# A step size that is written in place in PSUM, multiplied there, and then copied to SBUF

## The chip, the core and the metric

The kernel runs on one core of a Trainium2 chip. The metric is the device time of one execution in microseconds (us). Four runs of the kernel before took 8771.61 to 8812.8 us, with a median of 8785.41 us. The engines are named as in the profile: PE (TensorE, matrix multiply), DVE (VectorE), ACT (ScalarE), POOL (GpSimd) and SP (SyncE, which here only issues transfers).

## What is computed

Four images of 96 channels and 64 x 64 pixels pass through four layers: a selective state space model over the pixels (layer 0), a deformable convolution (layer 1), a Fourier layer and a feed-forward network (layer 2), and a linear attention with another feed-forward network (layer 3). The change lies in layer 0. Its core, cut from the reference:

```python
delta = softplus(dts + delta_bias)          # the step size, (batch, 4, 192, 4096)
# for every pixel, in each of 4 directions k:
dA = exp(delta[..., None] * A)              # A: 16 states for each of 192 channels
h  = dA * h + (delta * u)[..., None] * B
y  = einsum('bkdn,bkn->bkd', h, C)          # + D * u
```

`dts` is a small linear map of the layer's convolved input u. Two results of the step size are needed: delta itself, for the decay dA, and the product delta * u, for the inflow. The four directions are rows and columns, each forward and backward.

## The kernel before

**The scan.** `Layer0.scan` (L884) goes through 1536 units: image, direction, block of 1024 pixels, group of channels. For each unit, 8 channels by 16 states lie on the 128 partitions. ACT makes the decay `da` with an exponential (L1000) from a broadcast load of delta (L979); PE spreads the product into a PSUM tile `db` (L1006); DVE multiplies db by B (L1020, in place in PSUM) and runs the recurrence (L1028); POOL multiplies by C (L1037); PE sums over the states into `py` (L1056). A few units are in flight at a time.

**Beside the scan.** Everything else is written as Python generators and is put between the scan's instructions. There are two streams. Stream 0 (`ends`) makes the inputs of layer 0 for images 0 to 3 (`first`, `before`), and then takes each image through layers 2 and 3: Fourier layer (two halves, each hidden, transforms, and "last", L1576 to L1583), feed-forward network ("FFN", 8 chunks, L1643 to L1681), attention, FFN. Stream 1 (`middle`) finishes layer 0 of each image (`behind`) and does layer 1 (`Layer1`; the sampling gathers pixels with L1369 and ends in the matmuls L1402 and L1418). Image b can enter layer 2 only when stream 1 has sampled it.

**What sets the order.** A planner decides at build time what stands beside which unit. Each generator yields steps with an estimated work per engine (`cost(dve=0.7)`), and `pipe` (L273) lets a chain go on when the engines have room by its own clock (`Clock`). Steps can take and free named tiles (`takes`, `frees`), and can say that they hold a PSUM bank (`holds=1`). Beside the scan there are three banks for all streams (pool `mm`), and `has_bank` (L393) starts no new chain that needs a bank while three are held. The instructions of every engine then run in the order in which they were written out, each waiting only for its data. After the last unit the scan's banks are given to stream 0 (`own_banks`), and what is left of both streams is written out without a scan beside it. In that part the FFN uses DVE for its conversions; beside the scan it uses ACT and POOL.

**The step size.** `Layer0.steps` (L810) is called 192 times: 4 images, 8 pieces of 512 pixels, 6 combinations of directions and channels. Each call:

- L827: PE makes dts in the bank `pd` (128 x 512, one bank).
- L829 to L833: ACT makes exp(-|dts|) in `ex`, log(1 + ex) in `lw`, and 1 + ex in `w1`.
- L836: DVE forms the rounding error of 1 + ex; L838: POOL corrects lw with it.
- L840: DVE makes the step size max(dts, 0) + lw from pd and lw, and writes it to the SBUF tile `rl`. This is the last reader of pd, and the bank is free after it.
- L846 and L847, L853 or L859: DVE multiplies rl by u into ex. 64 calls are plain (L859, u in `xa`), 48 take the channels 128 to 191 of a row and a column direction (L859, u in `xc`), 16 take those of one orientation in two halves (L846, and L847 with u read with a stride), and 64 read u with a stride as columns (L853).
- L862: SP issues the store of rl to DRAM, from where L979 loads it later.
- L866 to L876: ex is split into three bf16 parts, by ACT and by PE with a bank `pr` (L869, L870, L873), and L880 stores them. The scan's `db` comes from these.

`pd`, `pr` and the banks of all other chains beside the scan are the same three banks in turn.

Of the kernel before, what the change touches and what calls it, by code (L numbers as in the profile page):

```python
# [15 lines left out]
ALU = mybir.AluOpType  # L16
# [3 lines left out]
B, C, H, W = 4, 96, 64, 64  # L20
# [163 lines left out]
def cost(pe=0.0, dve=0.0, act=0.0, pool=0.0, **more):  # L184
    return Step((pe, dve, act, pool), **more)


def wait(us=0.0, **more):

    return Step((0.0,) * 4, us, **more)  # L190
# [75 lines left out]
class Chain:  # L266
    def __init__(self, steps, ready):
        self.steps, self.ready = steps, ready
        self.done, self.holds, self.new, self.takes = 0, 0, True, []
        self.kind = steps.gi_code  # L270


def pipe(net, chains, width, every=0, lane=None, **tiles):  # L273
# [5 lines left out]
    while True:  # L279
        if more and len(active) < width:  # L280
            steps = next(chains, None)
            if steps is None:
                more = False
            else:
                active.append(Chain(steps, clock.now()))
                continue
# [256 lines left out]
class Layer0:  # L543
# [266 lines left out]
    def steps(self, b, ks, j, us, dtw, sm, xdbl):  # L810

        net = self.net
        nc = net.nc
        cs = slice(j * CH, (j + 1) * CH)
        tk = f"{b}_{j}_" + "".join(str(k) for k in ks)
        both = len(ks) == 2

        def tile_of(name, bufs):
            return sm.tile([128, CH], F32, name=f"{name}{tk}", tag=name, bufs=bufs)

        yield wait(new=True, takes="ex lw")


        pd = net.mm(f"pd{tk}")
        for i, k in enumerate(ks):
            o, m = (pd[64 * i : 64 * i + 64], slice(128, DI)) if both else (pd, slice(0, 128))
            nc.tensor.matmul(o, lhsT=dtw[:, k, m], rhs=xdbl[k % 2, j], start=True, stop=True)  # L827
        ex = tile_of("ex", 3)
        nc.scalar.activation(ex, pd, AF.Abs)  # L829
        nc.scalar.activation(ex, ex, AF.Exp, scale=-1.0)  # L830
        lw, w1 = tile_of("lw", 1), tile_of("w1", 1)
        nc.scalar.activation(lw, ex, AF.Ln, bias=net.one)
        nc.scalar.activation(w1, ex, AF.Identity, bias=net.one)  # L833
        yield cost(pe=2.2 if both else 1.1, act=2.7, holds=1, takes="rl")
        rl = tile_of("rl", 2)
        nc.vector.scalar_tensor_tensor(w1, w1, -1.0, ex, ALU.add, ALU.subtract)  # L836
        yield cost(dve=0.7, holds=1)
        nc.gpsimd.tensor_sub(lw, lw, w1)  # L838
        yield cost(pool=1.3, holds=1)
        nc.vector.scalar_tensor_tensor(rl, pd, 0.0, lw, ALU.max, ALU.add)  # L840
        yield cost(dve=0.7, frees="lw")
        if both and ks[0] % 2 == ks[1] % 2:
            q, xc = ks[0] % 2, us[2]
            own, far = slice(64 * q, 64 * q + 64), slice(64 - 64 * q, 128 - 64 * q)
            turned = xc.rearrange("p (a b) -> p b a", a=64)
            nc.vector.tensor_mul(ex[own], rl[own], xc[own, cs])  # L846
            nc.vector.tensor_mul(  # L847
                ex[far].rearrange("p (a b) -> p a b", b=64),
                rl[far].rearrange("p (a b) -> p a b", b=64),
                turned[far, j * NR : (j + 1) * NR, :],  # L850
            )
        elif not both and ks[0] % 2:
            nc.vector.tensor_mul(  # L853
                ex.rearrange("p (w h) -> p w h", h=H),
                rl.rearrange("p (w h) -> p w h", h=H),
                us[1][:, j * NR : (j + 1) * NR, :],
            )
        else:
            nc.vector.tensor_mul(ex, rl, us[2 if both else 0][:, cs])  # L859
        parts = ((0, 64, ks[0], 128), (64, 128, ks[1], 128)) if both else ((0, 128, ks[0], 0),)  # L860
        for p0, p1, k, c0 in parts:
            nc.sync.dma_start(self.de_d[b][k][c0 : c0 + p1 - p0, cs], rl[p0:p1])  # L862
        yield cost(dve=0.7, takes="du", frees="rl")

        du = sm.tile([128, 3, CH], BF16, name=f"du{tk}", tag="du", bufs=2)
        nc.scalar.copy(du[:, 0, :], ex)  # L866
        yield cost(act=0.6, new=True)
        pr = net.mm(f"pr{tk}")
        nc.tensor.matmul(pr, lhsT=net.ident, rhs=ex, start=True, stop=False)  # L869
        nc.tensor.matmul(pr, lhsT=self.minus, rhs=du[:, 0, :], start=False, stop=True)  # L870
        nc.scalar.copy(du[:, 1, :], pr)
        yield cost(pe=1.5, act=0.6, holds=1, frees="ex")
        nc.tensor.matmul(  # L873
            pr, lhsT=self.minus, rhs=du[:, 1, :], start=False, stop=True, skip_group_check=True
        )
        nc.scalar.copy(du[:, 2, :], pr)  # L876
        yield cost(pe=0.4, act=0.6)
        for p0, p1, k, c0 in parts:
            dst = self.du_d[b][k][:, c0 : c0 + p1 - p0, cs]
            nc.sync.dma_start(dst.rearrange("s c t -> c s t"), du[p0:p1])  # L880
        self.ready.update((b, k, both, j) for k in ks)
        yield wait(frees="du")
# [979 lines left out]
```

## Time and profile before

| What | Value |
|---|---|
| Four runs, median | 8785.41 us |
| Profiled execution | 8801.28 us, its span 8799.5 us |
| Granted TensorE clock | 0.811 |
| PE busy | 6636.2 us (75%) |
| DVE busy | 6852.6 us (78%) |
| ACT busy | 4917.9 us (56%) |
| POOL busy | 5605.5 us (64%) |
| First and last L1028 begin | 200.8 and 7491.4 us |

The profile is of one execution. It gives for each engine the time in which it was busy, in slices of the span and in any stretch; groups of instructions by source line, with their shape, their count, the mean duration, and what ended the idle time before them; and a chain of waits that leads back from the last instruction. A wait is put down to whatever released it last. DVE is the busiest engine, but no engine is busy all the time, and the part up to 7494 us, with the scan, is unlike the part behind it.

### The profile page before, as it was taken

What the parts mean: (1) busy time and instruction counts of PE and PEld (TensorE: products, weight loads), DVE (VectorE), ACT (ScalarE), POOL (GpSimd) and SP (SyncE); (2) the same over time, 40 slices, a digit from 0 to 9 for tenths busy, and PEclk for the clock granted to TensorE, in tenths of its full rate; (3) what the DMA queues carried; (4) which work ended last, traced back from release to release, by engine and by line L of the source; (5) the groups of instructions that cost most, each with busy time, mean ns of one, the idle gap of its engine ahead of it and who ended that gap; (6) DMA issues with size and microseconds to landing.
All of it is one profiled execution on the core that took longest, in us unless ns stands there. A gap on an engine that the chain in (4) does not pass through costs nothing.

```text
span 8799.5 us, 96335 instructions
## 1 busy us (share of the span) xinstructions
PE 6636.2 (75%) x31960; PEld 2923.1 (33%) x31960; DVE 6852.6 (78%) x5155; ACT 4917.9 (56%) x9030; POOL 5605.5 (64%) x4291
## 2 busy tenths in 40 slices
PE   6765877678777777887666787877768887778697
PEld 2211221123232232221222354422325552367383
DVE  2799989989798988778999887788888778367414
ACT  4554566546577776555666765445676565322323
POOL 0565666666588887656688886666888776177000
PEclk8876887779787887877788788877878887888887
DMA  3566677877788888777788888767888787255110
GB/s 86 168 197 188 180 195 216 212 183 195 196 233 238 242 232 208 191 177 190 212 236 221 234 223 200 183 166 185 216 209 230 202 215 163 58 167 168 30 52 11
DMA packets 775990, 1608.41 MB, mean 183 GB/s; under 512 B 247809, under 2 KB 339357, under 8 KB 773382
## 3 DMA queue, kind: packets, MB, share of 16 engines
q10 hardware_dynamic: 244224, 843.17, 37.1%
q1 hardware_dynamic: 457542, 532.51, 22.4%
q0 software_dynamic: 73728, 226.57, 9.7%
q8 instruction: 257, 4.21, 0.2%
q14 instruction: 239, 1.96, 0.1%
HBM read 1345.62 MB, written 256.29 MB: 182 GB/s over the span
## 4 chain that ended last, share of the span: by engine, by line
PE 34%; DVE 30%; DMA 16%; ACT 8%; issue 7%; POOL 2%; SPq 1%; ACTq 1%; DVEq 0%; POOLq 0%
DVE hh L1028 15%; DVE db L1020 8%; DMA du<-du 4%; PE py L1056 4%; PE pc L750 4%; PE f L1496 3%; PE ps L1402 3%; PE db L1006 3%; DMA da<-de 2%; PE pd L1418 2%; ACT g L1381 2%; ACT da L1000 2%; DMA bc<-bcd 1%; PE h L1537 1%; PE py L1051 1%
## 5 line engine op out<-in xcount | busy, mean ns | idle before, releaser
L1037 POOL TENSOR_TENSOR hh<-hh,bc 128x1024 f32<-128x1024 f32 x1536 | 3658.7, 2384 | 384.8 <-DVE hh L1028 278.7
L1028 DVE TENSOR_TENSOR_SCAN hh<-da,st,db 128x1024 f32<-128x1024 f32 x1152 | 2701.1, 2345 | 192.5 <-PE py L1056 74.1
L1020 DVE TENSOR_TENSOR db<-db,bc 128x1024 f32<-128x1024 f32 x1536 | 1863.3, 1213 | 577.2 <-PE db L1006 575.9
L1000 ACT ACTIVATE da<-da,w_al 128x1024 f32<-128x1024 f32 x1536 | 1740.1, 1145 | 614.6 <-DMA da<-de 182.3
L1006 PE MATMUL db<-du,rep 96*128 96x512 bf16 x3072 | 1098.4, 446 | 890.4 <-DVE hh L1028 841.0
L1369 POOL DMA_INDIRECT g<-table,idx x1152 | 1213.9, 1054 | 371.0 <-issue 180.1
L1056 PE MATMUL py<-hh,w_fold 128*32 128x512 f32 x6144 | 1065.6, 768 | 9.5 <-issue 3.9
L1381 ACT ACTIVATE g<-g,wt 128x96 f32<-128x96 f32 x3456 | 963.8, 364 | 147.7 <-DVE hh L1028 50.6
L1028 DVE TENSOR_TENSOR_SCAN hh<-da,db 128x1024 f32<-128x1024 f32 x384 | 877.3, 2285 | 95.0 <-PE py L1056 42.3
L1006 PEld LDWEIGHTS <-rep 96*128 96x128 bf16 x3072 | 281.3, 106 | 1881.1 <-issue 1202.7
L1402 PE MATMUL ps<-w_ident,g 128*96 128x128 f32 x3744 | 686.1, 324 | 196.7 <-ACT g L1381 121.7
L838 POOL TENSOR_TENSOR lw<-lw,w 128x512 f32<-128x512 f32 x192 | 244.1, 1271 | 710.7 <-DVE w L836 683.3
L1402 PEld LDWEIGHTS ps<-w_ident,g 128*96 128x96 f32 x3744 | 488.7, 143 | 565.2 <-ACT g L1381 246.7
L1035 POOL COPY st<-hh 128x1 f32<-128x1 f32 x1152 | 235.3, 204 | 675.6 <-DVE hh L1028 638.7
L750 PE MATMUL pc<-pad,wc 96*128 96x512 f32 x1152 | 573.0, 631 | 11.8 <-DVE rl L840 3.5
L1410 ACT COPY st<-ps 96x384 f32<-96x384 f32 x384 | 179.7, 473 | 461.3 <-PE ps L1402 420.1
L869 PE MATMUL pr<-ex,w_ident 128*128 128x512 f32 x384 | 278.4, 815 | 144.2 <-DVE ex L859 77.8
L750 PEld LDWEIGHTS pc<-pad,wc 96*128 96x128 f32 x1152 | 221.1, 199 | 322.6 <-issue 285.6
L1056 PEld LDWEIGHTS py<-hh,w_fold 128*32 128x32 f32 x6144 | 155.9, 123 | 503.0 <-issue 367.8
L1418 PE MATMUL pd<-st,wdc 96*128 96x256 f32 x1152 | 291.5, 401 | 4.0 <-ACT st L1410 1.1
L827 PE MATMUL pd<-xd,w_dtw 103*64 103x512 f32 (+1 forms) x512 | 248.2, 740 | 52.5 <-DVE rl L840 30.4
L1505 ACT COPY d<-f 128x512 f32<-128x512 f32 x192 | 111.9, 583 | 306.2 <-PE f L1496 291.8
(252 smaller groups left out, 8834.6 us busy)
## 6 DMA issues: line engine op xcount, KB each, us to landing
da<-de ACTq DMA_DIRECT2D x1536, 512.0 KB
du<-du SPq DMA_DIRECT2D x512, 192.0 KB
bc<-bcd SPq DMA_DIRECT2D x128, 512.0 KB
du<-du SPq DMA_DIRECT2D x128, 384.0 KB
y<-yb SPq DMA_DIRECT2D x384, 128.0 KB
de<-rl SPq DMA_DIRECT2D x128, 256.0 KB
m<-in_dft SPq DMA_DIRECT2D x128, 256.0 KB
ad<-y ACTq DMA_DIRECT2D x192, 128.0 KB
```

What stands on the lines that cost most here:

```text
L750: nc.tensor.matmul(pp, lhsT=wc[:, q, g * 128 : (g + 1) * 128], rhs=pad[:, r0 + dy : r0 + dy + NR, dx : dx + W], start=(q == 0), stop=(q == 8),
L869: nc.tensor.matmul(pr, lhsT=net.ident, rhs=ex, start=True, stop=False)
L1000: self.net.nc.scalar.activation(u.da, u.da, AF.Exp, scale=self.al[:, a : a + 1])
L1006: self.net.nc.tensor.matmul(db[:, h, :], lhsT=self.rep[:96, u.s % 4, :], rhs=u.du[u.s // 4][:, h * CH : (h + 1) * CH], start=True, stop=True,)
L1020: self.net.nc.vector.tensor_mul(u.db, u.db, u.bc[:, 0, :])
L1028: nc.vector.tensor_tensor_scan(u.along(u.hh), u.along(u.da), u.along(u.db), first, ALU.mult, ALU.add)
L1037: self.net.nc.gpsimd.tensor_mul(u.hh, u.hh, u.bc[:, 1, :])
L1056: nc.tensor.matmul(py[p0 : p0 + 32], lhsT=self.fold[:, u.i, :], rhs=hc[:, h * CH : (h + 1) * CH], start=u.sums["add"] is None and u.i == 0 ...
L1369: nc.gpsimd.indirect_dma_start(out=g[:, k, :], out_offset=None, in_=self.tables[b % 2], in_offset=bass.IndirectOffsetOnAxis(ap=idx[:, n : ...
L1381: nc.scalar.activation(pixel, pixel, AF.Identity, scale=wt[:, n, c : c + 1])
L1402: nc.tensor.matmul(pt[:, k, :], lhsT=g[:, k, c * C : (c + 1) * C], rhs=net.ident, is_transpose=True, start=(c == 0), stop=(c == corners - 1),)
L1418: nc.tensor.matmul(po, lhsT=wdc[:, k, :], rhs=st[:, k, :], start=(k == 0), stop=(k == 8))
```

## The change

The step size is no longer written to rl but back into pd, in place. The product is made at once from pd and u, in the same step of the planner, which now counts 1.4 us of DVE where two steps counted 0.7 each. Only then ACT copies pd to rl, in a new step of 0.6 us; that copy is the bank's last reader. The tile rl is made there. Stores and the split of the product follow as before.

```diff
         yield cost(pe=2.2 if both else 1.1, act=2.7, holds=1, takes="rl")
-        rl = tile_of("rl", 2)
         nc.vector.scalar_tensor_tensor(w1, w1, -1.0, ex, ALU.add, ALU.subtract)
         yield cost(dve=0.7, holds=1)
         nc.gpsimd.tensor_sub(lw, lw, w1)
         yield cost(pool=1.3, holds=1)
-        nc.vector.scalar_tensor_tensor(rl, pd, 0.0, lw, ALU.max, ALU.add)
-        yield cost(dve=0.7, frees="lw")
+        nc.vector.scalar_tensor_tensor(pd, pd, 0.0, lw, ALU.max, ALU.add)
         if both and ks[0] % 2 == ks[1] % 2:
...
-            nc.vector.tensor_mul(ex[own], rl[own], xc[own, cs])
+            nc.vector.tensor_mul(ex[own], pd[own], xc[own, cs])
             nc.vector.tensor_mul(
                 ex[far].rearrange("p (a b) -> p a b", b=64),
-                rl[far].rearrange("p (a b) -> p a b", b=64),
+                pd[far].rearrange("p (a b) -> p a b", b=64),
                 turned[far, j * NR : (j + 1) * NR, :],
             )
         elif not both and ks[0] % 2:
             nc.vector.tensor_mul(
                 ex.rearrange("p (w h) -> p w h", h=H),
-                rl.rearrange("p (w h) -> p w h", h=H),
+                pd.rearrange("p (w h) -> p w h", h=H),
                 us[1][:, j * NR : (j + 1) * NR, :],
             )
         else:
-            nc.vector.tensor_mul(ex, rl, us[2 if both else 0][:, cs])
+            nc.vector.tensor_mul(ex, pd, us[2 if both else 0][:, cs])
+        yield cost(dve=1.4, holds=1, frees="lw")
+        rl = tile_of("rl", 2)
+        nc.scalar.copy(rl, pd)
+        yield cost(act=0.6)
         parts = ((0, 64, ks[0], 128), (64, 128, ks[1], 128)) if both else ((0, 128, ks[0], 0),)
         for p0, p1, k, c0 in parts:
             nc.sync.dma_start(self.de_d[b][k][c0 : c0 + p1 - p0, cs], rl[p0:p1])
-        yield cost(dve=0.7, takes="du", frees="rl")
+        yield wait(takes="du", frees="rl")
```

In the changed kernel the multiplies are L844 and L845, L851 and L857, and the copy is L860.

## Prediction

> **What bounds the kernel now.** I read the page's slices first, then a table of busy time by stretch, then the groups of instructions, and last the order in which the built programs' instructions stand.
>
> ```profile
> PE   6765877678777777887666787877768887778697
> ...
> DVE  2799989989798988778999887788888778367414
> ...
> ## 4 chain that ended last, share of the span: by engine, by line
> PE 34%; DVE 30%; DMA 16%; ACT 8%; issue 7%; POOL 2%; SPq 1%; ACTq 1%; DVEq 0%; POOLq 0%
> ```
>
> VectorE (DVE) is at 0.8 to 0.9 and more until slice 34 of 40, then falls, while PE stays where it was; the chain is shared between the two. So there are two stages. From 201 to 7494 us run the 1536 units of the scan (L1020, 1213 ns, then L1028, 2345 ns: 3.56 us of DVE for each, 4.75 us in fact). From 7494 us to the end, 1306 us, a tail without scan is led by PE. Now four stretches of the scan (columns: stretch, length, busy us and instructions of PE, weight loads, DVE, ACT, POOL; clock, DMA share, GB/s):
>
> ```profile
> 3500.00:4000.00 500.00, 409.70 (x1281) 135.65 (x1277) 381.92 (x246) 281.75 (x373) 303.22 (x219) 0.84 0.73 181
> 4000.00:4500.00 500.00, 343.76 (x1330) 113.80 (x1331) 462.17 (x324) 304.79 (x554) 356.15 (x275) 0.77 0.80 214
> 4500.00:5000.00 500.00, 357.61 (x1530) 144.12 (x1530) 448.48 (x290) 349.69 (x775) 425.16 (x334) 0.80 0.86 229
> 5000.00:5500.00 500.00, 396.76 (x2900) 237.89 (x2899) 394.31 (x266) 300.26 (x718) 380.78 (x302) 0.85 0.86 214
> ```
>
> They hold 101, 102, 113 and 103 scans. What a stretch needs beyond 3.56 us a scan is 140, 137, 98 and 133 us. Beyond its scans (3.56 us of DVE, some 1.55 us of PE each) it has DVE work of 22, 99, 46 and 28 us and PE work of 253, 186, 182 and 237 us. Stretches 2 and 3 differ in DVE by 53 us and in need by 39; stretches 1 and 3 differ in PE by 71 us and in need by 42, though 3 has more DVE. A straight line through all 15 stretches from 200 to 7500 us gives 0.5 us of time per us of DVE and 0.55 per us of PE; the pairs give 0.7 and more. I take **0.6 for both**: neither engine alone is the bound, and work on either costs a bit over half.
>
> **The change, part by part.**
>
> (1) **The multiply by u.** Before, it reads two SBUF tiles, rl and u (columns: busy us, mean ns, idle before and what ended it; then ns min/median/max).
>
> ```profile
> L853 DVE TENSOR_TENSOR ex<-rl,xa 128x512 f32<-128x512 f32 x64 | 99.3, 1552 | 2.0
> L859 DVE TENSOR_TENSOR ex<-rl,xa 128x512 f32<-128x512 f32 x64 | 77.6, 1212 | 2.0
> L859 DVE TENSOR_TENSOR ex<-rl,xc 128x512 f32<-128x512 f32 x48 | 49.7, 1036 | 1.4
> L840 DVE SCALAR_TENSOR_TENSOR rl<-pd,lw 128x512 f32<-128x512 f32 x192 | 130.1, 677 | 19.9 <-DMA de<-rl 10.2 <-POOL lw L838 9.6
> ```
> ```profile
> L859 DVE TENSOR_TENSOR ex<-rl,xa x64: 681/693/5826, 114.7 to 4997.6; 128x512 f32<-128x512 f32 x64
> L840 DVE SCALAR_TENSOR_TENSOR rl<-pd,lw x192: 659/679/692, 114.0 to 4995.8; 128x512 f32<-128x512 f32 x192
> L1600 DVE TENSOR_TENSOR tl<-tl,lnb x64: 655/682/685, 5069.1 to 8701.4; 96x512 f32<-96x512 f32 x64
> ```
>
> L859 takes 0.69 us as a rule and up to 5.8 us, more than a whole POOL multiply (L1037, 2384 ns). L840 and L1600, with one operand in PSUM, never take over 0.69, and L1020, which also writes PSUM in place, never over 1.30 at twice the size. So the stretching belongs to two SBUF operands beside a busy GpSimd, and a multiply with its first operand in PSUM should lose it. What goes: L853 64 x (1552-1040), for 1040 is its own floor with the strided u, which stays; L859 64 x (1212-691) and 48 x (1036-691); L846 16 x (1121-689); L847 16 x (1557-1041): 33+33+17+7+8 = **98 us of DVE**. At 0.6 that is **-59 us**, all of it between 110 and 5000 us; the ends are -45 and -98, if all of it is on the path. The in-place stt costs what L840 costs: 0.
>
> [...]
>
> (2) **The added copy.** 192 ScalarE copies PSUM to SBUF of 128x512; L1067 is the same thing at 574 ns: 110 us of ACT. ACT is busy some 0.62 of 1000 to 5000 us, so its idle time covers it; cost 0. Without that cover the exponentials L1000 would come late for the scan: all scans wait 18 us for them now (L1028 for ACT da). I keep 0 to +30. In the built program the copy waits for the multiply, so ScalarE's queue stands there; before it stood one instruction later, at L866, which waits for the same multiply (93 us in all). The stores of the step size start 1.3 to 1.6 us later; SP's queue holds transfers for scans tens of units ahead, so 0.
>
> (3) **The bank.** pd is released after stt, multiply and copy and not after stt: 0.69+0.58 to 1.04+0.58 us, say 1.5 us, later. What queues behind it is PE:
>
> ```profile
> PE pd L827 <- DVE rl L840: 30.4, 20, 5.1
> PE px L799 <- DVE rl L840: 26.5, 11, 3.6
> PE pr L869 <- DVE rl L840: 20.6, 3, 14.3
> PE po L1264 <- DVE rl L840: 17.7, 3, 6.5
> PE pr L869 <- DVE ex L859: 77.8, 36, 15.0
> ```
>
> Thirty-nine waits, 99 us, with L750's two. Each grows by 1.5: 59 us of PE. In the new order banks are also reused sooner: a bank left by pr is taken again within 12 instructions 50 times, not 26. Say 80 to 100 us in all. Against it stand 121 us in which PE waited for the product (L859, L853, L847), most of which is the stretching of (1): some 50 us go. Net +40 us of PE, at 0.6 **+25 us**; ends 0 and +60.
>
> (4) **The planner's order.** The bank is held one step more, three banks serve all streams, so the planner starts each chain later. By the built order the last step size of image 3 is made beside unit 1047 and not 1015, and all of that stream's later work slips with it. After the last scan there now also stand half of "last" of image 1's transform (64 L1576, 8 L1581, 56 L1496), a normalization, a whole FFN (8 chunks) and some 2 chunks of the out-projection. Out of the scan go DVE 8x1.26 + 8x0.68 + 8x1.11 + 2x0.67 + 2.2 = 28 us and PE, by the same counting with the mean of each line, 87 us; at 0.6 **-69 us** (ends -50 and -90).
>
> The tail takes them on. Its stretches now:
>
> ```profile
> 7493.00:7740.00 247.00, 176.90 (x633) 70.03 (x632) 88.23 (x154) 85.23 (x175) 55.22 (x49) 0.78 0.33 80
> 7740.00:8180.00 440.00, 383.97 (x3289) 310.78 (x3288) 300.94 (x397) 123.60 (x248) 313.23 (x270) 0.88 0.53 157
> 8320.00:8800.00 480.00, 392.03 (x3028) 275.82 (x3028) 127.10 (x217) 137.24 (x270) 3.83 (x1) 0.82 0.11 34
> ```
>
> Up to the first sampling matmul (7719 us) PE gets 45 us more; it has 70 us of idle in the first row, which hides a part: +33. While image 3 is sampled (to 8173 us) PE has 7 us less: -7. After it stream 0 runs alone: before, the rest of an FFN, attention, an FFN and image 3; now also a half "last", a normalization and three eighths of an FFN. Image 3's own second half shows their length alone: 8573 to 8616, 27 us, 3/8 of 34 us: +83. Sum **+109 us** (ends +85 and +135).
>
> **Sum**: -59 + 0 + 25 - 69 + 109 = +6 us. The profiled execution took 8801.28 us (span 8799.5), 16 above the median of 8785.41; the forecast is 8785 + 6 = **8791 us**. A difference under about 0.3%, 26 us, can't be told from no change here.
>
> **Rivals.**
>
> *Slower: the bank decides.* If not 39 but some 140 of 192 steps meet a PE instruction waiting for their bank, PE waits 100 x 1.5 = 150 us more (the growth of the old 39 is paid for by what is won back at L869), and at 0.6 that is +90: -59-69+109+90 = +71, **8856 us**. It decides from about 75 us of net PE waiting (+45, total +26). For it: hold time of pd in the new order rises from 2.8 to 3.9 units, reuse within 12 instructions doubles behind pr. Against: the planner knows the hold and delays the user in the order.
>
> *Faster: DVE is the bound where the steps are.* From 4000 to 5000 us it is 0.91 busy; if the 98 us pass whole, the banks cost nothing and the tail's first phase hides its part (+95): -98-69+95 = -72, **8713 us**. Against: the 0.5 of the fit.
>
> *It doesn't do what it says.* The multiply stretches as before, u being still in SBUF: -59 falls away and bank waits double: about 8875 us. L1600 and L1159 (tile and bank, at most 690 ns) speak against it.
>
> **How the numbers follow.** Balance (8755 to 8825) 0.37, of which 0.05 faster, 0.27 same, 0.05 slower; bank 0.33; DVE bound 0.25; not as said 0.05. That makes faster 0.30, same 0.27, slower 0.43. The terms' ends add up to -98+0-90+85 = -103 and -45+30+60-50+135 = +130, or 8682 and 8915; that all fall on one side together is unlikely, so I take 8705, just beyond the rival on that side, and 8880, which takes in both cases on the other. Balance alone is 8755 to 8825.
>
> **What would show it.** The multiplies at 0.68 us (L851 1.04) with no long maximum; 192 copies L860 at 0.58; last scan near 7494-103 = 7390 us, and a tail of about 1415 us, with 48 FFN chunks in it. A scan that ends near 7494 or later means that PE's or ScalarE's waits ate the gain: look at who waits for L860. A tail of 1306 means that (4) was wrong.

## The result, and the profile after

| | Before | After |
|---|---|---|
| Median | 8782.38 us (70 runs) | 8784.9 us (44 runs) |
| Lowest to highest | 8724.09 to 8814.21 us | 8751.34 to 8810.74 us |
| Ratio, 95% interval | | 1.0006 [0.9998, 1.0015] |
| Profiled execution, span | 8801.28, 8799.5 us | 8827.3, 8825.5 us |
| First and last scan begin | 200.8, 7491.4 us | 195.2, 7423.7 us |

The change makes no difference that can be told from none: the time after lies between 0.02% below and 0.15% above, and 8791 us was forecast. The profiled execution of the changed kernel is some 40 us above its own median and above all of the 44 runs, so its trace is read for what happens, and times are taken from the ratios.

First the slices and the head of the chain, from the page of the changed kernel:

```profile
PE   6775877679677777887667778787777878779697
...
DVE  2698989888799998778898878888898876376414
...
## 4 chain that ended last, share of the span: by engine, by line
PE 36%; DVE 27%; DMA 17%; ACT 8%; issue 6%; POOL 2%; SPq 2%; ACTq 1%; DVEq 0%; POOLq 0%
```

VectorE now begins to fall a slice earlier, and in the chain DVE has lost three hundredths and PE has gained two, which fits less scan and more tail. Next the groups of the step size in the changed kernel (busy us, mean ns, idle before and its releaser), and the spread of single instructions (ns min/median/max; the last line is of the kernel before):

```profile
L835 DVE SCALAR_TENSOR_TENSOR w<-w,ex 128x512 f32<-128x512 f32 x192 | 198.8, 1035 | 130.7 <-ACT w L833 120.1 <-DMA bcd<-xd 10.4
L839 DVE SCALAR_TENSOR_TENSOR pd<-pd,lw 128x512 f32<-128x512 f32 x192 | 131.6, 686 | 9.9 <-POOL lw L837 9.9
L851 DVE TENSOR_TENSOR ex<-pd,xa 128x512 f32<-128x512 f32 x64 | 67.1, 1049 | 2.2
L857 DVE TENSOR_TENSOR ex<-pd,xa 128x512 f32<-128x512 f32 x64 | 44.3, 691 | 2.2
L857 DVE TENSOR_TENSOR ex<-pd,xc 128x512 f32<-128x512 f32 x48 | 33.2, 691 | 1.6
```
```profile
L857 DVE TENSOR_TENSOR ex<-pd,xa x64: 691/691/693, 115.4 to 5098.9; 128x512 f32<-128x512 f32 x64
L851 DVE TENSOR_TENSOR ex<-pd,xa x64: 1019/1042/1127, 526.2 to 5037.5; 128x512 f32<-128x512 f32 x64
L853 DVE TENSOR_TENSOR ex<-rl,xa x64: 1012/1060/3168, 531.5 to 4917.5; 128x512 f32<-128x512 f32 x64
```

The plain multiply (L857) now takes 691 to 693 ns; its longest was 5826 ns. The one with the strided u (L851) takes 1019 to 1127 ns; its longest was 3168. All five forms of the multiply together take 172.1 us instead of 269.4. One group of the step size got longer: L835, which is L836 of the kernel before (854 ns), has a mean of 1035. It reads two SBUF tiles, as the multiply used to, and is stretched beside the same GpSimd: 48 of the 192 took over 1.3 times the shortest, 665 ns, and 46 of these overlap a GpSimd multiply (L1039) in the trace; before it was 22, all beside that multiply (L1037 there).

Who waits for whom, in the changed kernel from 110 to 5100 us (engine, its tile and line, what it waited for: us in all, times, longest), and what the added copy itself waited for (us, times):

```profile
PE pr L875 <- ACT du L873: 88.7, 77, 9.5
PE pr L872 <- ACT du L868: 85.8, 38, 18.4
...
PE pr L871 <- DVE ex L851: 14.6, 8, 4.0
...
PE pr L871 <- DVE ex L857: 10.7, 5, 4.1
...
PE pr L871 <- ACT rl L860: 8.4, 3, 4.6
...
PE pz L774 <- ACT rl L860: 3.8, 3, 1.9
```
```profile
L860 ACT COPY rl<-pd x192: 558/576/609, 118.4 to 5104.7; 128x512 f32<-128x512 f32 x192
...
its engine sat idle before it (us, times) until:
  DVE ex L857: 58.6, 23
  DVE ex L851: 18.5, 9
```

The copy, now the bank's last reader, holds up PE for some 16 us (8.4 and 3.8 in the lines above, the rest in waits under 2 us), where the step size L840 held it up for 99; its weight loads wait 43 us for the copy and waited 101 for L840. The product is waited for 25 us instead of 121. In exchange PE waits longer for the casts of the split: 89 and 86 us, which before, as L873 waiting for L871 and L870 for L866, were 60 and 41 us. ScalarE is a little later with them.

Last the tail of both kernels (stretch, length, busy us and instructions of PE, weight loads, DVE, ACT, POOL; clock, DMA share, GB/s): before the sampling of image 3, during it, and after it; first the kernel before, then the changed one.

```profile
7494.00:7719.00 225.00, 169.89 (x620) 67.20 (x620) 76.91 (x140) 82.67 (x169) 36.78 (x35) 0.80 0.28 65
7719.00:8173.00 454.00, 385.15 (x3281) 311.97 (x3282) 304.74 (x395) 122.01 (x244) 329.88 (x282) 0.86 0.55 164
8173.00:8799.00 626.00, 493.14 (x3353) 319.18 (x3351) 196.06 (x342) 193.90 (x392) 11.23 (x3) 0.83 0.10 29
```
```profile
7426.00:7694.00 268.00, 210.44 (x850) 99.92 (x849) 86.25 (x147) 91.51 (x184) 53.71 (x49) 0.78 0.37 80
7694.00:8148.00 454.00, 379.17 (x3162) 296.99 (x3161) 313.92 (x428) 126.94 (x254) 318.67 (x271) 0.86 0.53 157
8148.00:8825.00 677.00, 528.36 (x3578) 335.32 (x3576) 221.94 (x380) 216.09 (x435) 11.49 (x3) 0.86 0.09 28
```

The scan ends at 7426 instead of 7494 us and the tail is 1399 instead of 1306 us long: +43, 0 and +51. (The first execution lies 19 us above its kernel's median, the second 42.) Work has moved from beside the scan to behind it, as forecast.

### The profile page after: what moved, and what is told of

Its sections match the earlier page's. It is cut to its first block, busy times and chain, and to the rows that moved or that the text cites. A ratio compares the mean times of both kernels' runs of the same rounds, so it can differ in the third digit from the quotient of the medians.

```text
span 8825.5 us, 96220 instructions
## 1 busy us (share of the span) xinstructions
PE 6642.1 (75%) x31960; PEld 2931.7 (33%) x31960; DVE 6794.7 (77%) x5203; ACT 4987.2 (57%) x9190; POOL 5533.6 (63%) x4275
## 4 chain that ended last, share of the span: by engine, by line
PE 36%; DVE 27%; DMA 17%; ACT 8%; issue 6%; POOL 2%; SPq 2%; ACTq 1%; DVEq 0%; POOLq 0%
DVE hh L1030 14%; DVE db L1022 7%; PE py L1058 4%; DMA du<-du 4%; PE pc L750 4%; PE f L1498 3%; PE db L1008 3%; PE ps L1404 3%; DMA da<-de 3%; PE pd L1420 2%; ACT g L1383 2%; POOL hh L1039 1%; ACT da L1002 1%; PE h L1539 1%; PE py L1053 1%
## 5 line engine op out<-in xcount | busy, mean ns | idle before, releaser
L1039 POOL TENSOR_TENSOR hh<-hh,bc 128x1024 f32<-128x1024 f32 x1536 | 3633.6, 2367 | 411.4 <-DVE hh L1030 290.7
L1022 DVE TENSOR_TENSOR db<-db,bc 128x1024 f32<-128x1024 f32 x1536 | 1864.2, 1214 | 530.9 <-PE db L1008 528.9
L1404 PE MATMUL ps<-w_ident,g 128*96 128x128 f32 x3744 | 710.1, 329 | 239.8 <-ACT g L1383 144.0
L1037 POOL COPY st<-hh 128x1 f32<-128x1 f32 x1152 | 217.6, 189 | 716.6 <-DVE hh L1030 677.4
L837 POOL TENSOR_TENSOR lw<-lw,w 128x512 f32<-128x512 f32 x192 | 243.8, 1270 | 670.8 <-DVE w L835 648.0
L871 PE MATMUL pr<-ex,w_ident 128*128 128x512 f32 x384 | 269.8, 792 | 47.7 <-DVE ex L851 14.6
L835 DVE SCALAR_TENSOR_TENSOR w<-w,ex 128x512 f32<-128x512 f32 x192 | 198.8, 1035 | 130.7 <-ACT w L833 120.1
```

What stands on the lines that cost most here:

```text
L1022: self.net.nc.vector.tensor_mul(u.db, u.db, u.bc[:, 0, :])
L1039: self.net.nc.gpsimd.tensor_mul(u.hh, u.hh, u.bc[:, 1, :])
L1404: nc.tensor.matmul(pt[:, k, :], lhsT=g[:, k, c * C : (c + 1) * C], rhs=net.ident, is_transpose=True, start=(c == 0), stop=(c == corners - 1),)
```

## The experiments

A total that hits says little when five terms of both signs make it up, so each term was tested by itself. They were run in three groups, each on a chip of its own, on which the kernel before had medians of 8755.26 (E1 to E4), 8854.5 (E5 to E8) and 8862.35 us (E9 to E12); all are compared by their ratio to it. The changed kernel itself was not run on these three chips, so where an experiment is set against it, or against one of another group, a ratio has to carry over from chip to chip. It does so only roughly: with the changed order the tail took 1399 us in the changed kernel, 1384 and 1387 in E2 and E3 (first group), but 1476 in E8 and 1483 in E12 (second and third). "Multiplies" is the busy time of the five forms.

| | Kernel | Ratio to before [95%] | Median us | Multiplies us |
|---|---|---|---|---|
| | after | 1.0006 [0.9998, 1.0015] | 8784.9 | 172.1 |
| E1 | new instructions, old order | 1.0102 [1.008, 1.0125] | 8849.13 | 171.2 |
| E2 | old instructions, new order | 1.0093 [1.0065, 1.0121] | 8833.17 | 315.8 |
| E3 | after without L835 | 0.996 [0.9944, 0.9977] | 8713.5 | 172.3 |
| E4 | copy in the multiply's step | 1.0133 [1.0111, 1.0155] | 8875.28 | 171.2 |
| E5 | copy in the cast's step | 0.9957 [0.9938, 0.9977] | 8821.01 | 171.9 |
| E6 | E5, cast before copy | 0.9997 [0.9978, 1.0017] | 8840.1 | 171.7 |
| E7 | old instructions, idle ACT copy in E1's place | 1.0175 [1.0149, 1.0201] | 9009.52 | 287.9 |
| E8 | after, copy made twice | 1.0046 [1.0027, 1.0065] | 8899.08 | 172.5 |
| E9 | E2 without the longer hold | 1.0022 [1.0006, 1.0039] | 8883.36 | 308.8 |
| E10 | old instructions, steps merged | 1.0046 [1.0029, 1.0063] | 8905.35 | 278.1 |
| E11 | old instructions, E5's order | 1.0075 [1.0045, 1.0106] | 8930.69 | 307.2 |
| E12 | after without the matmuls L875 | 0.9987 [0.9971, 1.0003] | 8851.45 | 172.3 |

**E1: the new instructions in the old order.** rl is made where it was, and the copy goes into the step that the step size had; all queues but ScalarE's keep the order of the kernel before. Against the changed kernel:

```diff
-        yield cost(dve=1.4, holds=1, frees="lw")
-        rl = tile_of("rl", 2)
         nc.scalar.copy(rl, pd)
-        yield cost(act=0.6)
+        yield cost(dve=0.7, frees="lw")
...
-        yield wait(takes="du", frees="rl")
+        yield cost(dve=0.7, takes="du", frees="rl")
```

> The changed instructions (step size in place in the bank, multiply from the bank, ScalarE copy) written out in the old order: multiply and copy stand in the same planner step as the step size, so that every queue but ScalarE's (192 copies more) is as before; the tail holds the same 40 FFN chunks. The planner doesn't know that the bank is busy longer. Theory on record (multiplies lose their stretching, worth -59; banks cost +25 to +35): 8740 to 8755 against 8782 before. Rival 1, the stretching only moves on to the next VectorE instruction with two SBUF operands, L836: its mean rises by over 150 ns, DVE loses some 58 us of busy time and not 98, and the time is 8755 to 8780. Rival 2, VectorE is the bound here: 8685 to 8700.

Measured: 1.0102; all the figures missed, and on the same side. What the copy waited for, in this kernel's trace:

```profile
L859 ACT COPY rl<-pd x192: 563/586/597, 115.7 to 5075.0; 128x512 f32<-128x512 f32 x192
...
its engine sat idle before it (us, times) until:
  DVE ex L858: 213.6, 84
  DVE ex L852: 169.6, 48
  DVE ex L846: 42.5, 14
```

ScalarE's queue stands 426 us at the copy, for VectorE has not made the product yet when ScalarE arrives. Everything behind it is late: VectorE waits 202.5 us for L833 (123.6 before), PE 183.0 us for the first cast L867 (40.9). So the gain of the multiplies is there (171.2 us) and ScalarE's waiting eats it. That became the new theory, "the queue": the place of the copy in ScalarE's order costs more than its 110 us of work. Its rival, "the bank", lays E1's price on the bank, which is free only after the copy. E4 ran beside E1; E5 to E7 were made to tell the two apart.

**E2: the old instructions in the new order.** The instructions of the kernel before with the steps of the change, an empty step of ScalarE among them. Against the kernel before:

```diff
-        yield cost(dve=0.7, frees="lw")
...
+        yield cost(dve=1.4, holds=1, frees="lw")
+        yield cost(act=0.6)
...
-        yield cost(dve=0.7, takes="du", frees="rl")
+        yield wait(takes="du", frees="rl")
```

> The old instructions (rl in SBUF, no copy) with the planner steps of the change: one step of 1.4 us of DVE that holds the bank, then a step of 0.6 us of ACT in which nothing is done. The order is that of the changed kernel, 48 FFN chunks behind the last scan. Theory on record: scan 69 us shorter, tail 109 us longer, 8822 (8810 to 8835). Rival 1 (the change's own instructions gain little, and order costs little): 8780 to 8795. Rival 2 (order costs what the multiplies gain, 98): 8865 to 8885.

Measured: 1.0093, some 82 us at a median of 8782 (57 to 106 by its interval). The theory on record, 8822 or 1.0046, missed; rival 2, 1.0095 to 1.0117, comes nearest. The scan ends at 7450 us in its profile and the tail is 1384 us long; in E1, on the same chip and with the old order, it is 7559 and 1290. The order alone costs, and it is also bad for the old multiplies. Its groups:

```profile
L852 DVE TENSOR_TENSOR ex<-rl,xa 128x512 f32<-128x512 f32 x64 | 104.3, 1629 | 2.2
L858 DVE TENSOR_TENSOR ex<-rl,xa 128x512 f32<-128x512 f32 x64 | 88.8, 1387 | 2.3
L858 DVE TENSOR_TENSOR ex<-rl,xc 128x512 f32<-128x512 f32 x48 | 69.8, 1455 | 1.7
```

They were 1552, 1212 and 1036 ns: the same instructions are stretched more in this order. In one and the same order the change takes off 315.8 - 172.1 = 144 us, not the 98 that the profile of before shows, and 1.0093 - 1.0006 = 0.87%, some 76 us (50 to 102 with both intervals, on two chips).

**E3: VectorE work taken out.** The changed kernel without the 192 L835 (199 us); ScalarE writes zeros in their place.

```diff
-        nc.scalar.activation(w1, ex, AF.Identity, bias=net.one)
+        nc.scalar.mul(w1, ex, 0.0)
...
-        nc.vector.scalar_tensor_tensor(w1, w1, -1.0, ex, ALU.add, ALU.subtract)
```

> The changed kernel without the 192 VectorE instructions L835 that form the rounding error of 1+ex; ScalarE writes zeros to w1 in their place, so log(1+ex) stays uncorrected. Planner steps are unchanged, so is the order. Measures what a microsecond of VectorE beside the scan is worth: these instructions are busy 199 us. Rate 0.6 as on record: 8785-119 = 8666 (8640 to 8690). VectorE is the bound (rate 1): 8585 to 8610. VectorE hardly matters (rate 0.2): 8745.

Measured: 0.996, 0.46% below the changed kernel, about 40 us (24 to 57 with both intervals, on two chips) for 199 us of VectorE: 0.2 us for one, not 0.6. The groups show the rest as waiting:

```profile
L1021 DVE TENSOR_TENSOR db<-db,bc 128x1024 f32<-128x1024 f32 x1536 | 1864.4, 1214 | 595.2 <-PE db L1007 592.8
L838 DVE SCALAR_TENSOR_TENSOR pd<-pd,lw 128x512 f32<-128x512 f32 x192 | 131.8, 686 | 83.9 <-POOL lw L836 83.9
```

After the change these two lines stood idle for 530.9 and 9.9 us. Of 175 us of VectorE that went (6794.7 to 6619.8), 138 came back as waits at PE's spread and at GpSimd's subtraction.

**E4: the copy in the multiply's own step.** The copy directly behind the multiply, no step of its own, bank held:

```diff
-        yield cost(dve=1.4, holds=1, frees="lw")
-        rl = tile_of("rl", 2)
         nc.scalar.copy(rl, pd)
-        yield cost(act=0.6)
+        yield cost(dve=1.4, holds=1, frees="lw")
```

> The changed instructions with multiply and copy in the one planner step of 1.4 us of DVE that holds the bank, and no step of ScalarE behind it. By the built order the last step size then stands beside unit 952 (1012 before, 1044 in the changed kernel), and the tail loses a normalization and half of an attention's keys and values, 43 us of PE. If the slip of the order comes from the step of ScalarE and not from the held bank, this has the gain of the instructions and none of the longer tail: 31 us below e1_old_order, 8710 to 8725 by the theory on record, 8725 to 8750 by rival 1, 8655 to 8670 by rival 2.

Measured: 1.0133; here too all the figures missed. Its tail is only 1222 us long, the shortest of all, and it is still the slowest with the new instructions: ScalarE stands 450 us at the copy (212.3 until L858, 195.1 until L852, 42.7 until L846). So a tail that is 68 us shorter than in E1 (1290 us, same chip) doesn't help while the copy stands in that place.

**E5: the copy later.** Two steps for VectorE as before, both holding the bank, and the copy in the one step that ScalarE had already, in front of the cast. Against the changed kernel:

```diff
         nc.vector.scalar_tensor_tensor(pd, pd, 0.0, lw, ALU.max, ALU.add)
+        yield cost(dve=0.7, holds=1, frees="lw")
...
-        yield cost(dve=1.4, holds=1, frees="lw")
+        yield cost(dve=0.7, holds=1, takes="du")
         rl = tile_of("rl", 2)
         nc.scalar.copy(rl, pd)
-        yield cost(act=0.6)
...
-        yield wait(takes="du", frees="rl")
...
         nc.scalar.copy(du[:, 0, :], ex)
-        yield cost(act=0.6, new=True)
+        yield cost(act=1.2, new=True, frees="rl")
```

> The changed instructions, but the copy stands in the planner's existing ScalarE step, just ahead of the product's bf16 cast, and step size and product keep their two steps of 0.7 us of DVE. No step is added, the bank is held through two more steps. By the built order the tail is that of the kernel before (40 FFN chunks, last step size beside unit 1015 against 1012), and ScalarE finds the product ready. Theory of the queue (the price of the copy is ScalarE's queue standing at it, 426 us in e1_old_order, and the changed kernel avoids that by a step of its own that makes the tail longer): the gain of the multiplies is left, 8755 before minus 45 to 75 = 8680 to 8710. Theory of the bank (its longer hold costs): no better than before, 8755 to 8830.

Measured: 0.9957 [0.9938, 0.9977], faster than both kernels, though by 0.43% and not by the 0.5 to 0.9% that the queue theory gave. The multiplies are as short as in the changed kernel, and ScalarE stands 41.5 us where it stood 77 after the change (L857 and L851) and 426 in E1. The copy's own view:

```profile
L861 ACT COPY rl<-pd x192: 559/576/604, 118.1 to 5004.0; 128x512 f32<-128x512 f32 x192
...
its engine sat idle before it (us, times) until:
  DVE ex L858: 41.5, 21
```

**E6: the bank 0.6 us longer.** E5 with the cast of the product ahead of the copy, so that the bank goes back one ScalarE instruction later:

```diff
+        du = sm.tile([128, 3, CH], BF16, name=f"du{tk}", tag="du", bufs=2)
+        nc.scalar.copy(du[:, 0, :], ex)
         nc.scalar.copy(rl, pd)
...
-        du = sm.tile([128, 3, CH], BF16, name=f"du{tk}", tag="du", bufs=2)
-        nc.scalar.copy(du[:, 0, :], ex)
```

> As e5_copy_later, with the cast of the product ahead of the copy of the step size in ScalarE's queue. PE waits for the cast, and 0.58 us later for the bank. Theory of the queue: 0 to 15 us below e5_copy_later. Theory of the bank: 5 to 15 us above it.

Measured: 0.9997; 0.4% above E5 by the ratios, on the same chip 19 us by the medians and 28 by the means of 12 runs each (11 to 46 at 95%). PE's wait for the copy at L869 is 49.2 us, in E5 18.5. So the bank has a price where its next user stands right behind it; its size stays rough.

```profile
PE pr L869 <- ACT rl L863: 49.2, 18, 13.4
```

**E7: only ScalarE's wait.** The instructions of the kernel before, in E1's order, with a useless copy by ScalarE of the product into w1 at the place where E1 has its copy. The bank is free as early as ever. Against the kernel before:

```diff
-        yield cost(dve=0.7, frees="lw")
...
+        nc.scalar.copy(w1, ex)
+        yield cost(dve=0.7, frees="lw")
```

> The kernel before (step size in SBUF, bank free after it, multiplies with two SBUF operands) in the order of e1_old_order, with a ScalarE copy that nobody needs at the place of the changed kernel's copy: it copies the product ex to w1 and so waits for the multiply. Theory of the queue: the whole price of e1_old_order (94 us over before) and the lost gain of the multiplies, 8755+94+50 = 8900 (8880 to 8930). Theory of the bank: the bank is free early here, so only 8755 to 8775.

Measured: 1.0175, as the queue theory has it (8900 from 8755 is 1.0166); the bank theory's 1.002 falls. Little of this can be the work of the copies, which E8 below puts at some 50 us at most: 1.75% is 155 us. Idle before the copy, in this trace:

```profile
L859 ACT COPY w<-ex x192: 602/618/636, 115.2 to 5152.2; 128x512 f32<-128x512 f32 x192
...
its engine sat idle before it (us, times) until:
  DVE ex L858: 240.8, 68
  DVE ex L852: 186.9, 47
  DVE ex L846: 56.5, 14
```

E1 against E7, the same order and the same place: 0.73%, some 64 us, for 117 us less of multiplies and a bank held longer.

**E8: the copy twice.** The changed kernel with a second copy behind the first.

```diff
         nc.scalar.copy(rl, pd)
+        nc.scalar.copy(rl, pd)
```

> The changed kernel with the copy of the step size made twice, one after the other; the planner doesn't know of the second, so the order is the same. ScalarE is busy 110 us more. If its idle time covers the copy (record): 0 to 20 us above the changed kernel, which is 1.0006 of before, so 8760 to 8780. If ScalarE's time counts as PE's and VectorE's (0.6): 8825.

Measured: 1.0046, 0.40% or some 35 us (17 to 53 with both intervals) above the changed kernel, for 110 us of ScalarE (the second copy also holds the bank 0.58 us longer). Whether that is the copy's price isn't shown, for the two ran on different chips. All copies are made before 5120 us, and yet the last scan begins no later (first the changed kernel, then E8):

```profile
L1030 DVE TENSOR_TENSOR_SCAN hh<-da,st,db x1152: 2319/2347/2364, 363.3 to 7423.7; 128x1024 f32<-128x1024 f32 x192
L1031 DVE TENSOR_TENSOR_SCAN hh<-da,st,db x1152: 2316/2346/2452, 366.0 to 7409.5; 128x1024 f32<-128x1024 f32 x192
```

The tail, which has no copies, is 1476 instead of 1399 us long. The profiles don't settle it either, as that of the changed kernel is 42 us above its median. So the price of the copies lies somewhere between nothing and some 50 us.

**E9 and E10: which part of the steps costs.** Both have the instructions of the kernel before. E9 is E2 without the hold (the edit below, against E2); E10 is E9 without the empty step `cost(act=0.6)`.

```diff
-        yield cost(dve=1.4, holds=1, frees="lw")
+        yield cost(dve=1.4, frees="lw")
```

> The old instructions in the planner steps of the change, but without the bank's longer hold: one step of 1.4 us of DVE, then an empty step of 0.6 us of ACT. By the built order the last step size stands beside unit 1051 and 48 FFN chunks are left behind the scan, as with the hold. Theory of the step (the slip of the order, and its price, come from the step of ScalarE): 1.007 to 1.011 of before, as e2_order_only (1.0093). Theory on record (the hold): 0.998 to 1.002.

> The old instructions, with step size and product in one planner step of 1.4 us of DVE and no step of ScalarE behind it. The last step size stands beside unit 980 and 41 FFN chunks are left, the tail is that of before. Theory of the step: 0.998 to 1.002 of before. Rival: the merged step puts the multiply beside POOL more often (in e2_order_only the 208 multiplies were busy 316 us against 269 before), and that is the price of the order: multiplies above 300 us and 1.004 to 1.009.

Measured: E9 1.0022, E2 with the hold 1.0093. So most of the order's price hangs on the bank that the planner thinks is held one step more (the two on different chips). The hold doesn't make the whole slip of the order, though. Without it E9 still has its last step size beside unit 1051 and 48 FFN chunks in its tail; E10, without the empty step, has it beside unit 980 and 41 chunks. What the hold adds behind the scan is the half "last" and a normalization: 640 matmuls of the transform (L1576) stand in the tails of E2 and of the changed kernel, 512 in those of E9, E10 and the kernel before. E10's 1.0046 lies in the range of its rival, but the rival's cause is not there: the multiplies take 278.1 us and not over 300. What makes it slower than E9 is open.

**E11: E5's order with the old instructions.**

```diff
-        yield cost(dve=0.7, frees="lw")
+        yield cost(dve=0.7, holds=1, frees="lw")
...
+        yield cost(dve=0.7, holds=1, takes="du")
...
-        yield cost(dve=0.7, takes="du", frees="rl")
...
-        yield cost(act=0.6, new=True)
+        yield cost(act=1.2, new=True, frees="rl")
```

> The old instructions in the planner steps of e5_copy_later (bank held two steps more, a ScalarE step of 1.2 us in which only the cast is made). Order as there. e5_copy_later is 0.9957 of before; what this kernel has above that is the worth of the instructions in that order. If the multiplies' stretching (98 us) counts 0.6 and the copy costs a third of its 110 us: +0.3%, so 0.998 to 1.001. If the order itself was the gain of e5_copy_later: 0.994 to 0.997.

Measured: 1.0075, above both figures expected. E5's gain is therefore no gift of its order, which by itself is worse than the old one; the instructions are worth 1.0075 - 0.9957 = 1.18%, some 104 us (the two on different chips). The multiplies of this kernel are as long as in E2 and E9:

```profile
L853 DVE TENSOR_TENSOR ex<-rl,xa 128x512 f32<-128x512 f32 x64 | 110.3, 1724 | 1.9
L859 DVE TENSOR_TENSOR ex<-rl,xa 128x512 f32<-128x512 f32 x64 | 76.0, 1188 | 2.0
L859 DVE TENSOR_TENSOR ex<-rl,xc 128x512 f32<-128x512 f32 x48 | 66.4, 1383 | 1.5
```

**E12: PE work taken out.** The changed kernel without the 192 matmuls L875 (84 us of PE).

```diff
-        nc.tensor.matmul(
-            pr, lhsT=self.minus, rhs=du[:, 1, :], start=False, stop=True, skip_group_check=True
-        )
```

> The changed kernel without the 192 matmuls L875 that form the remainder for the third bf16 part (the third part then holds the second remainder unreduced). They are busy 84 us on PE, and PE waits 89 us for the cast in front of them. Measures what PE time is worth beside the scan; the changed kernel is 1.0006 of before. Rate 0.6 as on record: -50 us, 0.995. Rate 0.2, as VectorE showed in e3_no_w1 (40 us for 199): -17 us, 0.9985. If the wait of PE's queue counts too: -100 us, 0.989.

Measured: 0.9987, 0.19% below the changed kernel, some 17 us for 84: 0.2 us for one, with an interval that reaches almost to nothing. As with E8 the chips differ, and the profile has another figure:

```profile
L1027 DVE TENSOR_TENSOR_SCAN hh<-da,st,db x1152: 2314/2346/2365, 361.5 to 7364.0; 128x1024 f32<-128x1024 f32 x192
```

The last scan begins 60 us earlier than in the changed kernel, which would be 0.7 us for one, and the tail is 1483 us long instead of 1399, though none of these matmuls stand there. What PE's time is worth beside the scan stays open.

## Why the prediction came out right, point by point

The forecast was +6 us, the ratio says +5. The cause was the one forecast, a gain on VectorE against a loss by the order, but no term had its right size, and that the errors cancel to within 1 us is luck. By the runs, from the ratios at 8782 us:

| Term | Predicted us | By the runs us | From |
|---|---|---|---|
| (1) multiplies | -59 | -76 to -111 | E2 to after is -76; -111 if the copy costs E8's 35 |
| (2) copy | 0 | 0 to +35 | E8, not secure |
| (3) bank | +25 | not seen apart | waits for L860 |
| (4) order | -69 + 109 = +40 | +82 | E2 |
| Sum | +6 | +6 (the ratio: +5) | |

The sum on the right is no check: the first row is what is left when E2, E8 and the change are set against each other, and E8 prices a second copy, not the first. What the runs do give are two figures, each some 25 us either way: the new order costs 82 us, and the new instructions in it, terms (1) to (3) together, gain 76. Predicted were 40 and -59 + 0 + 25 = -34. Both were some 42 us too small, in opposite directions. The prediction did not lean on its sum either: it gave a slower kernel a chance of 0.43 and the same time 0.27.

**(1) The mechanism held, the size did not.** A first operand in PSUM ends the stretching, in three pairs of one order each (E2 and after, E7 and E1, E11 and E5): in the changed kernel the plain multiply takes 693 ns at most and the strided one 1127, and in E1 and E5 their means are at most 692 and 1048. What was mis-sized is the stretching: the profile of before showed 98 us, but in the changed order it would have been 144. And "0.6 for both" was a slope over stretches in which everything varies together. A shorter multiply gives 76/144 = 0.5 to 111/144 = 0.8 after E2, 64/117 = 0.5 from E7 to E1, and 104/135 = 0.8 to (104 + 35)/135 = 1.0 from E11 to E5, the higher figures with E8's price of the copy; these are rough, each gain by some 30 us. Work that is simply taken out gives 0.2 in E3, which leans on the changed kernel's ratio from another chip; from E2 to E3, on one chip, 289 us less of VectorE gave 1.33% or 117 us, 0.4 for one with the copies paid. The multiply stands between the step size and everything that follows it, while L835 stands ahead of a GpSimd instruction that takes longer than itself (L837, 1270 ns); that this makes the difference is an argument, not shown. Reading PSUM costs the plain multiply nothing that the traces show: its median is 691 ns with the first operand there (L857 after the change) and 693 with both in SBUF (L859 before).

**(2) "its idle time covers it; cost 0" is neither confirmed nor refuted.** E8 has 35 us, about the upper bound of 30 that was kept, but that can be the chip's. (Two readings in the working were a little off: ScalarE was busy 0.64 of 1000 to 5000 us, not 0.62, and the scans waited 16 us for the exponentials, not 18.) What the runs do show is that the place decides. The working saw the danger, that the copy waits for the multiply and ScalarE's queue stands there, but set it aside, since "before it stood one instruction later, at L866": E1, E4 and E7 show that with the copy in the wrong step ScalarE stands 426 to 484 us at it, and these kernels are 1.0 to 1.75% slower than the one before. In the change, where the copy has a step of its own behind the product, it waits only 81 us.

**(3) The bank's price came in another place.** PE's waits for the bank fell from 99 us to 16; they did not grow. Why they fell so far is open: with the old instructions in the new order they are 72 us (E2), and without the planner's hold 63 (E9), so the planner's delay of the next user, which stood in the prediction against the rival "the bank decides", does not explain it. What the hold costs sits in the order (1.0093 in E2, 1.0022 in E9, on two chips). Where the copy comes one ScalarE instruction later, as in E6, the wait appears.

**(4) The tail was about right, the scan's gain was not.** The slip comes only in part from the held bank, which the prediction named as its reason: the step size and the FFN move with the added step of ScalarE, the half "last" and a normalization with the hold (E9, E10). Predicted were a tail of about 1415 and a scan's end at 7390 us; the profile has 1399 and 7426, in an execution 42 us above its median. The phase before the sampling was put at +33 and is +43, the one after it at +83 and is +51. The half "last" that came into it was costed at 42 us from its like in the profile of before and took 27, at a granted clock of 1.00 and not 0.54, as the last section shows; that is 15 of the 32 us. But the work that left the scan gave back little: E2's tail is 94 us longer than E1's, which has the old order on the same chip, and E2 as a whole loses 82 us, so some 12 us came back and not 69. Some of E2's 82 us is the longer stretching (46 us more of multiplies), which the changed kernel does not have; row (1) is larger for the same reason.

**The rivals.** "The bank decides" would have given 1.008; "DVE is the bound" 0.992, and E3 shows that VectorE as such is not the bound. "It doesn't do what it says" fell with 691 ns. That the stretching only moves on, to L835 beside the same GpSimd, was a theory after the profile: 1035 ns after, 916 in E2. But the same order has 929 in E8 and 978 in E12. In pairs of one order, old and new instructions, it is 916 and 929 to 1035 (E2 and the three with the changed order), 859 and 927 (E7, E1), and 931 and 936 (E11, E5). So L835's mean varies from kernel to kernel; that the change adds up to 0.12 us to each of the 192, 23 us in all, is not excluded.

## What to carry to other kernels

An operation moved to another engine should be costed by what its queue does at that point, not by that engine's idle share: with the same 192 copies of 0.58 us a kernel was 0.43% faster than before (E5) or 1.0 to 1.3% slower (E1, E4), by the planner's steps in which they stood in ScalarE's order. Where a planner sets the order, its estimates and holds are part of the change: run the old instructions in the new order, and the new ones in the old. Here that took a change of nothing apart into a gain and a loss, and keeping the gain with a cheaper place for the copy (E5) gave a kernel 0.43% faster than before.

## What the runs showed of the hardware

**The multiply with one operand in PSUM did not stretch.** With two operands in SBUF the plain multiply took 681 to 5826 ns, with the first in PSUM 691 to 693; the strided one took 1012 to 3168 and 1019 to 1127. Of the 208 multiplies of the kernel before, 67 took over 1.3 times the shortest of their line, and each of the 67 overlaps a GpSimd multiply (L1037) in the trace. Of the 112 plain ones after the change, 85 overlap one too (L1039) and stay within 691 to 693 ns. The strided multiply's last 0.1 us, up to 1127 ns, is unexplained. The order alone changed the stretching, from 269 us of multiplies to 316 (E2).

**The same work at two clocks.** Half a "last" in the tail of the kernel before, and the one that the change moved there:

```profile
8573.00:8615.00 42.00, 35.14 (x144) 24.79 (x144) 9.34 (x8) 5.13 (x9) 0.00 (x0) 0.54 0.08 26
```
```profile
8150.00:8176.00 26.00, 20.31 (x151) 15.44 (x149) 9.34 (x8) 4.64 (x8) 0.00 (x0) 1.00 0.14 45
```

The second row lies some 2 us too early: it has a few matmuls of the sampling and misses the last two of the half "last". From its first matmul to the end of its last addition the half takes 42.2 us in the first kernel (8573.5 to 8615.7) and 26.9 in the second (8151.6 to 8178.5). The additions on VectorE (L1583, after L1585) take 1.23 to 1.28 us each in both. Sixteen of the matmuls L1576 (after L1578) take 2.7 us in the stretch with the granted clock of 0.54, but for the first sixteen with 1.6, and 1.5 in the one with 1.00. So the 42.2 us, read at 0.54, did not carry over to the place at 1.00.
